# First layer of a four-layer kernel: softmax weights turned by VectorE in 32x32 blocks, values as 32x64 tiles, four engines in a written order

## The chip, the cores and the metric

The kernel runs on one core of one Trainium2 chip. Its engines work side by side and meet through semaphores: TensorE (PE in the profile, with its weight loads shown apart as PEld), VectorE (DVE), ScalarE (ACT), GpSimd (POOL), and the queues that start transfers, of which SyncE (SP) does nothing else. The metric is the time of one execution on the device in microseconds. Three runs of the kernel before gave 3634.38, 3636.60 and 3638.72 us, so the median is 3636.6 us.

## The reference, cut to what matters

Four layers are computed one after the other for a batch of eight sequences. The change touches the first layer only. For each batch b it has two inputs x[b] and ctx[b], read as 256 channels by 512 positions. Queries, keys and values of 16 heads with 64 channels each are linear maps of x and ctx, by matrices of which each is made of blocks that act on the two halves of the positions. Then, per head:

```
scores = (q + r_w_bias)^T k          # 512 x 512, per head
probs  = softmax(scores / 8, over keys)
av     = v probs^T                   # 64 x 512, per head
z      = Wo [av of 16 heads] + bo + x    # 256 x 512
out    = (z - mean) * rsqrt(var + eps)   # over the 256 channels
```

The result of each batch is stored in DRAM and read by the second layer. All arithmetic is fp32.

## The kernel before, in words

`stage_l0` (from line 117) does the first layer. The unit of work is a **pair**: two heads (128 rows of channels) of one batch. There are 8 batches x 8 pairs = 64 pairs. A pair has 512 queries, cut into four quarters of 128; two quarters are a slot, so the layer has 128 slots.

**Groups.** The linear maps are computed by a Strassen-like scheme: a group makes q and k of one pair (kind "qk", 8 per batch) or a quarter of v of one batch (kind "v", 4 per batch). A group has four parts. `load_w` (line 146) issues two transfers of 512 KB. `weight_sums` (line 220) makes four sums of weight blocks, s1 and s3 on POOL (lines 233, 234), s2 and s4 on DVE (235, 236). `group` (257) and `group2` (268) run seven products on TensorE into PSUM banks, four in `group` and three in `group2`, and combine them by additions on DVE and POOL (lines 261 to 298). Each fp32 matmul stands in the trace as two matmul instructions with a weight load each.

**Softmax.** `scores` (300) makes, for each quarter, two matmuls (line 308), the negated row maximum (DVE, 312), its scaling by 1/8 (DVE, 313), two exponentials with row sums (ACT, 317), the reciprocal (DVE, 322) and the scaling of both heads (POOL, 324).

**Turning.** The values need the weights with keys on the partitions. `transposes` (330) turns 128x128 blocks on TensorE against an identity (338) into PSUM, and `evac` copies them to SBUF, alternately on DVE (174) and ACT (172).

**Values.** `values` (343) runs, per slot, eight fp32 matmuls with 128 keys as contraction, two heads side by side in the columns of the array (352); DVE copies the result to SBUF (356). `out_proj` (358) follows once per batch, then the norm (`norm_sum`, `norm_mean`, `norm_var`) and `store`.

**Order.** Only TensorE's order is written by hand: the loop at line 452 runs the scores of the next slot, the values of the last one, pieces of other groups taken from a list with due positions (`Filler`, `put_group`), and the transposes of this slot. The other engines' order is chosen by the framework. The transfers of weights go through SP's queue. In the last slots of the layer, the first steps of the second layer (`g.middle.fill`) are mixed in.

PSUM has eight banks: two score tiles of two banks each (tag "s"), and four banks with the tag "mm" that products, transposes, values and projections share in turn.

Of the kernel before, what the change touches and what calls it, by code (L numbers as in the profile page):

```python
# [116 lines left out]
def stage_l0(g, pools):  # L117
# [11 lines left out]

    nc, tc, I = g.nc, g.tc, g.I  # L130
# [15 lines left out]
    def load_w(kind, b, i, ts=(0, 1), eng=nc.sync):  # L146

        for t in ts:
            shape = [P, 4, ST, P] if kind == "qk" else [P, 2, ST, 256]
            w = g.wpool.tile(shape, F32, tag="w", name="w" + kind)  # L150
            raw.setdefault((kind, b, i), []).append(w)
            eng.dma_start(out=w, in_=I["wqk"][i, t] if kind == "qk" else I["wv"][i // 2, i % 2, t])
# [9 lines left out]
    nc.scalar.dma_start(out=WoT, in_=I["WoT"].rearrange("(k p) o -> p k o", p=P))  # L162
# [3 lines left out]
    qs, ks, vs, avs, sms, pts = {}, {}, {}, {}, {}, {}  # L166
# [10 lines left out]
    def qk_first(b, pr, t):  # L177
# [10 lines left out]
        if t == 0:  # L188
            q = qs[b, pr] = wk.tile([P, L], F32, tag="q", name="q", bufs=2)
            nc.vector.tensor_scalar(q, pp, g.pv("rwb", pr), None, ALU.add)  # L190
        else:
            k_ = ks[b, pr] = wk.tile([P, L], F32, tag="k", name="k", bufs=2)
            nc.scalar.copy(k_, pp)

    def act_sums(b):

        z, u = (x.rearrange("p k (h i l) -> p i k h l", h=2, i=2) for x in (X[b], us[b]))
        t = {n: wk.tile([P, ST, 2, P], F32, tag="ts", name=f"t{n}", bufs=8) for n in (1, 2, 3, 4)}
        sub = lambda e, *a: tc.keep_in_program_order(e.tensor_tensor(*a, ALU.subtract))
        for e, n, x, y in (  # L200
            (nc.gpsimd, 1, z[:, 1], z[:, 0]), (nc.gpsimd, 3, u[:, 1], z[:, 1]),
            (nc.vector, 2, u[:, 1], t[1]), (nc.vector, 4, u[:, 0], t[2]),
        ):
            for k in range(ST):
                sub(e, t[n][:, k], x[:, k], y[:, k])
                yield
# [13 lines left out]
    def weight_sums(kind, b, i):  # L220
# [11 lines left out]
        s1, s2, s3, s4 = (wk.tile(shape, F32, tag="ws", name=f"s{n}", bufs=7) for n in (1, 2, 3, 4))  # L232
        nc.gpsimd.tensor_tensor(s1, a21, a22, ALU.add)
        nc.gpsimd.tensor_tensor(s3, a11, a21, ALU.subtract)
        nc.vector.tensor_tensor(s2, s1, a11, ALU.subtract)
        nc.vector.tensor_tensor(s4, a12, s2, ALU.subtract)
# [20 lines left out]
    def group(kind, b, i):  # L257
# [7 lines left out]
        nc.vector.tensor_tensor(u2, b2[:, 1], s15[:, 0], ALU.add)  # L265
        groups[kind, b, i] = out, s15, u2

    def group2(kind, b, i):
# [3 lines left out]
        x, y = s15[:, 0], wk.tile([P, 256], F32, tag="u3", name="u3", bufs=1)  # L272
        nc.gpsimd.tensor_tensor(x, u2, s15[:, 1], ALU.add)
        nc.vector.tensor_tensor(y, b3[:, 0], u2, ALU.add)
        add(kind, i, out[1], b3[:, 1], x, True)
        add(kind, i, out[2], b4[:, 0], y, False)
        add(kind, i, out[3], y, s15[:, 1], False, nc.gpsimd)

    def blocks(kind, b, i):

        if kind == "qk":
            q = qs[b, i] = wk.tile([P, L], F32, tag="q", name="q", bufs=2)
            k_ = ks[b, i] = wk.tile([P, L], F32, tag="k", name="k", bufs=2)
            return [
                t.rearrange("p (h i l) -> p i h l", h=2, i=2)[:, j] for t in (q, k_) for j in range(2)
            ]
        if i % 2 == 0:
            vs[b, i // 2] = wk.tile([P, 4, 512], F32, tag="vT", name="vT", bufs=2)
        t = vs[b, i // 2]
        return [t[:, 2 * (i % 2) + j, o * 256 : o * 256 + 256] for o in range(2) for j in range(2)]  # L290

    def add(kind, i, out, x, y, biased, eng=nc.vector):
        if kind == "qk":
            x, y = (t.rearrange("p (h l) -> p h l", h=2) for t in (x, y))
# [5 lines left out]
    def scores(b, pr, hf):  # L300
        out = []
        for j in range(2):
            it = 2 * hf + j
            ic = slice(it * P, (it + 1) * P)
            sp = ps.tile([P, 2, L], F32, tag="s", name="sp", bufs=2)
            for h in range(2):
                r = slice(h * DH, (h + 1) * DH)
                nc.tensor.matmul(  # L308
                    sp[:, h, :], lhsT=qs[b, pr][r, ic], rhs=ks[b, pr][r, :], start=True, stop=True
                )  # L310
            nmax = sm.tile([P, 2], F32, tag="nmax", name="nmax")
            nc.vector.tensor_reduce(nmax, sp, AX.X, ALU.max, negate=True)  # L312
            nc.vector.tensor_scalar(nmax, nmax, 1.0 / DH ** 0.5, None, ALU.mult)  # L313
            pe = wk.tile([P, 2, L], F32, tag="pe", name="pe", bufs=4)
            ssum = sm.tile([P, 2], F32, tag="ssum", name="ssum")
            for h in range(2):
                nc.scalar.activation(  # L317
                    pe[:, h, :], sp[:, h, :], AF.Exp, bias=nmax[:, h : h + 1], scale=1.0 / DH ** 0.5,
                    accum_out=ssum[:, h : h + 1],
                )  # L320
            rinv = sm.tile([P, 2], F32, tag="rinv", name="rinv")
            nc.vector.reciprocal(rinv, ssum)  # L322
            for h in range(2):
                nc.gpsimd.tensor_scalar(  # L324
                    pe[:, h, :], pe[:, h, :], rinv[:, h : h + 1], 1.0, ALU.mult, ALU.mult
                )
            out.append(pe)
        sms[b, pr, hf] = out

    def transposes(b, pr, hf, h):  # L330
        pes = sms[b, pr, hf]
        pt = pts[b, pr, hf, h] = wk.tile([P, 4, 2, P], F32, tag="pt", name="pt", bufs=3)
        for j2 in range(2):
            tp = ps.tile([P, 2, 2, P], F32, tag="mm", name="tp", bufs=4)
            for j in range(2):
                jt = 2 * j2 + j
                for i in range(2):
                    nc.tensor.transpose(  # L338
                        tp[:, j, i, :], pes[i][:, h, jt * P : (jt + 1) * P], g.ident
                    )  # L340
            evac(pt[:, 2 * j2 : 2 * j2 + 2], tp)

    def values(b, pr, hf):
        pt = [pts.pop((b, pr, hf, h)) for h in range(2)]
        if hf == 0:
            avs[b, pr] = wk.tile([P, L], F32, tag="av_sb", name="av_sb", bufs=8)
        av = ps.tile([P, 256], F32, tag="mm", name="av", bufs=4)
        vT = vs[b, pr // 4]
        for jt in range(4):
            for h in range(2):  # L350
                col = (2 * (pr % 4) + h) * DH
                nc.tensor.matmul(  # L352
                    av[h * DH : (h + 1) * DH, :], lhsT=vT[:, jt, col : col + DH],
                    rhs=pt[h][:, jt].rearrange("p i c -> p (i c)"), start=(jt == 0), stop=(jt == 3),
                )
        nc.vector.tensor_copy(avs[b, pr][:, hf * 256 : hf * 256 + 256], av)  # L356

    def out_proj(b, mt):
        zb = X[b]
        op = ps.tile([P, L], F32, tag="mm", name="op", bufs=4)  # L360
        for p in range(NP):
            nc.tensor.matmul(
                op, lhsT=WoT[:, p, mt * P : (mt + 1) * P], rhs=avs[b, p],
# [3 lines left out]
            zb[:, mt, :], op, g.pv("bo", mt), zb[:, mt, :], ALU.add, ALU.add  # L367
# [4 lines left out]
    def norm_sum(b):  # L372
        zb = X[b]
        rows[b] = wk.tile([P, L], F32, tag="rs", name="zs", bufs=1)
        nc.gpsimd.tensor_tensor(rows[b], zb[:, 0, :], zb[:, 1, :], ALU.add)

    def norm_mean(b):
# [4 lines left out]
        sq = wk.tile([P, ST, L], F32, tag="sq", name="sq", bufs=1)  # L382
        for k in range(ST):
            nc.vector.tensor_tensor(zb[:, k, :], zb[:, k, :], mp, ALU.subtract)
            nc.gpsimd.tensor_tensor(sq[:, k, :], zb[:, k, :], zb[:, k, :], ALU.mult)
        nc.gpsimd.tensor_tensor(sq[:, 0, :], sq[:, 0, :], sq[:, 1, :], ALU.add)
        rows[b] = sq[:, 0, :]

    def norm_var(b):
# [3 lines left out]
        rs = wk.tile([P, L], F32, tag="rs", name="rs", bufs=1)  # L393
        nc.scalar.activation(rs, vp, AF.Ln, bias=g.eps)
        nc.scalar.activation(rs, rs, AF.Exp, scale=-0.5)
        for k in range(ST):
            nc.gpsimd.tensor_tensor(zb[:, k, :], zb[:, k, :], rs, ALU.mult)
# [5 lines left out]
    def slot(b, pr, hf):  # L403
        return (b * NP + pr) * 2 + hf
# [4 lines left out]
    def put_group(at, *of):  # L409
        if of not in raw:  # L410
            fill.put(at - 6, lambda: load_w(*of))
        fill.put(at - 1.4, lambda: weight_sums(*of))
        fill.put(at + 0.2, lambda: group(*of))
        fill.put(at + 0.5, lambda: group2(*of))

    for b in range(B):
        s = slot(b, 0, 0)
        if b:
            fill.put(s - 13, lambda b=b: load_u(b))
            steps = act_sums(b)  # L420
            for n in range(9):
                fill.put(s - 8.6 + 0.5 * n, lambda steps=steps: next(steps))
            put_group(s - 3, "qk", b, 0)
        put_group(s - (4 if b else 2.8), "v", b, 0)
        put_group(s - (2 if b else 1.4), "v", b, 1)
        for i, at in ((1, -1), (2, 0), (3, 3), (4, 5), (5, 7), (6, 9), (7, 11)):
            put_group(s + at, "qk", b, i)
        put_group(s + 4, "v", b, 2)
        put_group(s + 6, "v", b, 3)
        for mt in range(ST):  # L430
            fill.put(slot(b + 1, 0, 1) + 0.2 + 0.2 * mt, lambda b=b, mt=mt: out_proj(b, mt))
        fill.put(slot(b + 1, 1, 0) + 0.4, lambda b=b: norm_sum(b))
        fill.put(slot(b + 1, 2, 0) + 0.4, lambda b=b: norm_mean(b))
        fill.put(slot(b + 1, 3, 0) + 0.4, lambda b=b: norm_var(b))
        fill.put(slot(b + 1, 4, 0) + 0.4, lambda b=b: store(b))
# [1173 lines left out]
```

## Time and profile before

| what | before |
|---|---|
| median of three runs | 3636.6 us |
| the profiled execution's own time | 3634.69 us |
| its span | 3632.9 us |
| granted TensorE clock, mean | 0.982 |
| first scores matmul (line 308) / last values matmul (line 352) start | 28.1 / 1480.3 us |
| time of one batch in the steady part | 183.0 us |
| in such a batch: PE, DVE, POOL, ACT busy | 183.0, 117 to 119, 106 to 108, 74 us |
| transferred in that part | 79 to 81 GB/s; in the first 50 us 233 GB/s |

The page of the profile gives busy shares per engine, the span in 40 slices, and groups of instructions by line. In a row of a group stand the line, the engine, the operation, what is written and read, the count, then the busy time and the mean duration of one, and at the end the idle time of the engine before them with what released it. The durations of neighbouring instructions overlap, so the pace of a stretch is read from the starts in the timeline, not from the mean duration.

### The profile page before, as it was taken

What the parts mean: (1) busy time and instruction counts of PE and PEld (TensorE: products, weight loads), DVE (VectorE), ACT (ScalarE), POOL (GpSimd) and SP (SyncE); (2) the same over time, 40 slices, a digit from 0 to 9 for tenths busy, and PEclk for the clock granted to TensorE, in tenths of its full rate; (3) what the DMA queues carried; (4) which work ended last, traced back from release to release, by engine and by line L of the source; (5) the groups of instructions that cost most, each with busy time, mean ns of one, the idle gap of its engine ahead of it and who ended that gap; (6) DMA issues with size and microseconds to landing.
All of it is one profiled execution on the core that took longest, in us unless ns stands there. A gap on an engine that the chain in (4) does not pass through costs nothing. (4 is left out here: it accounts for less than half of the span.)

```text
span 3632.9 us, 58189 instructions
## 1 busy us (share of the span) xinstructions
PE 3488.5 (96%) x22144; PEld 2500.9 (69%) x22144; DVE 2455.5 (68%) x3982; ACT 1495.9 (41%) x3616; POOL 2298.9 (63%) x2236
## 2 busy tenths in 40 slices
PE   8999999999999999889999998799999999899999
PEld 6777777777777777556666665466666666589996
DVE  5766575656565666488888887655676777677771
ACT  3434343434343434323333343355566665433222
POOL 5656565646464645356666566566777877688882
PEclk9999999999999999989999999899999999999999
DMA  4222222222222221212332223121121112300002
GB/s 170 85 86 82 76 82 76 83 71 84 73 82 76 82 65 47 93 58 64 111 99 93 91 95 110 53 80 62 55 70 56 52 48 73 114 1 1 1 7 87
DMA packets 102566, 263.13 MB, mean 72 GB/s; under 512 B 8400, under 2 KB 16464, under 8 KB 102288
## 3 DMA queue, kind: packets, MB, share of 16 engines
q1 hardware_dynamic: 98640, 252.21, 21.5%
q10 hardware_dynamic: 2992, 5.37, 0.4%
q8 instruction: 177, 2.90, 0.3%
q0 software_dynamic: 656, 1.81, 0.2%
q14 instruction: 101, 0.83, 0.1%
HBM read 238.39 MB, written 20.97 MB: 71 GB/s over the span
## 5 line engine op out<-in xcount | busy, mean ns | idle before, releaser
L324 POOL TENSOR_SCALAR pe<-pe,rinv 128x512 f32<-128x512 f32 x512 | 386.2, 766 | 466.7 <-DVE nmax L313 411.5
L317 ACT ACTIVATE pe<-sp,nmax 128x512 f32<-128x512 f32 x512 | 347.1, 683 | 601.7 <-DVE nmax L313 597.3
L793 POOL TENSOR_TENSOR rs<-a,r 128x1024 f32<-128x1024 f32 x128 | 303.2, 2384 | 261.1 <-DVE a L788 228.1
L1006 ACT ACTIVATE pe<-pe,nmax 128x256 f32<-128x256 f32 x512 | 253.7, 497 | 194.7 <-DVE nmax L999 194.0
L312 DVE TENSOR_REDUCE nmax<-sp 128x2 f32<-128x1024 f32 x256 | 310.8, 1214 | 8.9 <-PE sp L308 7.9
L1013 POOL TENSOR_SCALAR pe<-pe,rinv 128x256 f32<-128x256 f32 x512 | 236.9, 484 | 115.3 <-DVE rinv L1011 114.5
L788 DVE TENSOR_TENSOR_SCAN a<-w,vb 128x1024 f32<-128x1024 f32 x128 | 287.4, 2275 | 4.8
L308 PE MATMUL sp<-k,q 64*128 64x512 f32 x1024 | 254.7, 615 | 0.2 <-ACT pe L317 0.2
L338 PE MATMUL tp<-ident,pe 128*128 128x128 f32 x2048 | 249.8, 274 | 3.3 <-DVE av_sb L356 1.8
L352 PE MATMUL av<-pt,vT 128*64 128x256 f32 x2048 | 249.3, 385 | 0.0
L172 ACT COPY pt<-tp 128x512 f32<-128x512 f32 x256 | 147.7, 589 | 246.2 <-PE tp L338 246.2
L338 PEld LDWEIGHTS tp<-ident,pe 128*128 128x128 f32 x2048 | 227.1, 141 | 25.2 <-issue 14.8
L352 PEld LDWEIGHTS av<-pt,vT 128*64 128x64 f32 x2048 | 135.7, 136 | 151.6 <-DVE k L298 42.4
L999 DVE TENSOR_REDUCE nmax<-pe 128x4 f32<-128x1024 f32 x128 | 156.1, 1220 | 101.0 <-POOL pe L997 97.5
L249 PE MATMUL gp<-t,s 128*128 128x128 f32 x1512 | 204.9, 278 | 1.4 <-DVE vT L298 1.4
L249 PEld LDWEIGHTS gp<-t,s 128*128 128x128 f32 x1512 | 183.7, 192 | 5.6 <-DVE vT L298 1.6
L997 POOL TENSOR_TENSOR pe<-pe,lconstb 128x1024 f32<-128x1024 f32 x64 | 149.7, 2357 | 50.7 <-DVE pe L990 50.7
L322 DVE RECIPROCAL rinv<-ssum 128x2 f32<-128x2 f32 x256 | 42.4, 166 | 205.6 <-ACT pe L317 205.4
L174 DVE COPY pt<-tp 128x512 f32<-128x512 f32 x256 | 166.2, 679 | 1.5 <-PE tp L338 1.5
L1024 PE MATMUL tp<-ident,pe 128*128 128x128 f32 x1024 | 143.3, 287 | 23.1 <-POOL pe L1013 19.0
L997 POOL TENSOR_TENSOR pe<-pe,mb 128x1024 f32<-128x1024 f32 x64 | 149.7, 2361 | 18.1 <-DVE pe L990 18.1
L784 DVE TENSOR_TENSOR vb<-vb,k 128x1020 f32<-128x1020 f32 x128 | 157.2, 1228 | 4.4
(314 smaller groups left out, 8229.6 us busy)
## 6 DMA issues: line engine op xcount, KB each, us to landing
wqk<-in_wqk_dram SPq DMA_DIRECT2D x127, 512.0 KB, 3.5
wv<-in_wv_dram SPq DMA_DIRECT2D x62, 512.0 KB, 3.5
Wk<-in_l1WkT_dram SPq DMA_DIRECT2D x16, 512.0 KB, 4.1
Wv<-in_l1WvT_dram SPq DMA_DIRECT2D x16, 512.0 KB, 3.9
Wr<-in_l1WrT_dram SPq DMA_DIRECT2D x16, 512.0 KB, 4.2
Wg<-in_l1WgT_dram SPq DMA_DIRECT2D x16, 512.0 KB, 4.5
Wo<-in_l1WoT_dram SPq DMA_DIRECT2D x16, 512.0 KB, 4.2
fWk<-in_l1fWkT_dram SPq DMA_DIRECT2D x16, 512.0 KB, 4.2
```

Source lines behind the costliest of these rows:

```text
L249: nc.tensor.matmul(out[:, hf * P : (hf + 1) * P], lhsT=w[n](hf, k), rhs=a[n](hf, k), start=k == 0, stop=k == ST - 1,)
L308: nc.tensor.matmul(sp[:, h, :], lhsT=qs[b, pr][r, ic], rhs=ks[b, pr][r, :], start=True, stop=True)
L312: nc.vector.tensor_reduce(nmax, sp, AX.X, ALU.max, negate=True)
L317: nc.scalar.activation(pe[:, h, :], sp[:, h, :], AF.Exp, bias=nmax[:, h : h + 1], scale=1.0 / DH ** 0.5, accum_out=ssum[:, h : h + 1],)
L324: nc.gpsimd.tensor_scalar(pe[:, h, :], pe[:, h, :], rinv[:, h : h + 1], 1.0, ALU.mult, ALU.mult)
L338: nc.tensor.transpose(tp[:, j, i, :], pes[i][:, h, jt * P : (jt + 1) * P], g.ident)
L352: nc.tensor.matmul(av[h * DH : (h + 1) * DH, :], lhsT=vT[:, jt, col : col + DH], rhs=pt[h][:, jt].rearrange("p i c -> p (i c)"), start=(jt ...
L788: nc.vector.tensor_tensor_scan(a.rearrange("p n l -> p (n l)"), w4.rearrange("p n l -> p (n l)"), vb[:, 4 * n2 : 4 * n2 + 4, :].rearrange( ...
L793: nc.gpsimd.tensor_tensor(rs, a, rb, ALU.mult)
L997: nc.gpsimd.tensor_tensor(pe4, pe4, b4, ALU.add)
L1006: nc.scalar.activation(pe[:, r, :], pe[:, r, :], AF.Exp, bias=nmax[:, r : r + 1], accum_out=ssum[:, r : r + 1],)
L1013: nc.gpsimd.tensor_scalar(pe[:, r, :], pe[:, r, :], rinv[:, r : r + 1], 1.0, ALU.mult, ALU.mult)
```

## The change

It rewrites what lies between scores and output projection, and the order of the layer.

- `transposes` is gone. `turn` runs one VectorE instruction per quarter: it turns each 32x32 block of the [128, 1024] tile in place of blocks, into SBUF. Row block r of 32 partitions then holds, for its own 32 queries of each quarter, the keys of one block of 32 on the partitions.
- k is written with its positions permuted (`blocks`, `add`, `qk_first`), so that a block of 32 keys is every sixteenth key.
- `values` works on a whole pair: for 16 key blocks, 4 row groups and 2 heads one fp32 matmul with 32 keys, 64 channels and 4 x 32 queries. The four row groups write four PSUM banks, all that the tag "mm" has, and four copies (two on DVE, two on ACT) bring them to SBUF.
- Each row group needs all keys on its own 32 partitions. So v goes to DRAM (`store_v`) and `load_v` reads 256 KB four times per pair.
- Softmax is cut into `scores`, `exp`, `norm`, `norm2`. The scaling of the maximum moves to ACT. Head 0 is scaled by POOL, head 1 by ACT.
- The weight sums s2 and s4 move from DVE to POOL, in two steps. The output projection runs in halves of 256 columns. One small tile (u3) is gone; s15 still has one buffer.
- TensorE, VectorE, ScalarE and GpSimd all run in the order in which the program issues. Positions in the list are thirds of a pair (24 to a batch). The load of WoT moves from ACT's queue at the start to SP's queue at position 9.9.

```diff
+        nc.gpsimd.tensor_tensor(s2, s1, a11, ALU.subtract)
...
+        nc.gpsimd.tensor_tensor(s4, a12, s2, ALU.subtract)
...
+    def norm():
+        pe, ssum, of = exps.pop(0)
+        rinv = sm.tile([P, 2], F32, tag="rinv", name="rinv")
+        nc.vector.reciprocal(rinv, ssum)
+        nc.gpsimd.tensor_scalar(pe[:, 0, :], pe[:, 0, :], rinv[:, 0:1], 1.0, ALU.mult, ALU.mult)
+        halves.append((pe, rinv, of))
+
+    def norm2():
+        pe, rinv, of = halves.pop(0)
+        nc.scalar.mul(pe[:, 1, :], pe[:, 1, :], rinv[:, 1:2])
+        probs.append((pe, of))
+
+    def turn():
+        pe, (b, pr, it) = probs.pop(0)
+        if it == 0:
+            pts[b, pr] = wk.tile([P, 4, 2, L], F32, tag="pt", name="pt", bufs=1)
+        nc.vector.transpose(pts[b, pr][:, it], pe)
...
+    def load_v(b, pr):
+        vr = vrs[b, pr] = wk.tile([P, 16, P], F32, tag="vr", name="vr", bufs=2)
+        for r in range(4):
+            tc.keep_in_program_order(nc.sync.dma_start(
+                out=vr[32 * r : 32 * r + 32],
+                in_=vd[b, pr // 4][pr % 4].rearrange("(k n) c -> k n c", n=16),
+            ))
+
+    def values(b, pr):
+        pt, vr = pts.pop((b, pr)), vrs.pop((b, pr))
+        av = [ps.tile([P, 4, 32], F32, tag="mm", name="av", bufs=4) for _ in range(4)]
+        for kb in range(16):
+            for r in range(4):
+                rows_ = slice(32 * r, 32 * r + 32)
+                for h in range(2):
+                    nc.tensor.matmul(
+                        av[r][h * DH : (h + 1) * DH], lhsT=vr[rows_, kb, h * DH : (h + 1) * DH],
+                        rhs=pt[rows_, :, h, 32 * kb : 32 * kb + 32], start=(kb == 0), stop=(kb == 15),
                     )
...
+        for r in range(4):
+            evac(t.rearrange("p (i r q) -> p r i q", i=4, r=4)[:, r], av[r])
...
     for n, at in enumerate(every):
...
+        nxt, t = every[n + 1] if n + 1 < len(every) else None, 3 * n
+        exp()
+        norm()
+        norm2()
+        turn()
+        fill.until(t + 1.5)
+        if nxt:
+            for it in range(2):
+                scores(*nxt, it)
+                exp()
+            norm()
+        values(*at)
+        if nxt:
+            norm2()
+            norm()
+            norm2()
+            scores(*nxt, 2)
+            exp()
+            turn()
+            turn()
+            fill.until(t + 2.2)
+            norm()
+        fill.until(t + 2.5)
+        if nxt:
+            norm2()
+            scores(*nxt, 3)
+            turn()
+        fill.until(t + 2.95)
...
-    with stack, tc.manual_schedule(engines={mybir.EngineType.PE}):
+    every = {getattr(mybir.EngineType, n) for n in ("PE", "DVE", "Activation", "Pool")}
+    with stack, tc.manual_schedule(engines=every):
         stage_l0(g, pools)
```

## The prediction

> **What bounds the kernel now.** I read the page first, then the busy time of three successive batches, then the groups by line, then the timeline of one slot, and last one short stretch of the second layer.
>
> ```profile
> PE 3488.5 (96%) x22144; PEld 2500.9 (69%) x22144; DVE 2455.5 (68%) x3982; ACT 1495.9 (41%) x3616; POOL 2298.9 (63%) x2236
> PE   8999999999999999889999998799999999899999
> ...
> 213.00:396.00 183.00, 182.90 (x1240) 134.28 (x1238) 119.35 (x239) 74.09 (x176) 107.61 (x126) 1.00 0.26 81
> 396.00:579.00 183.00, 183.00 (x1242) 134.45 (x1240) 117.18 (x238) 74.12 (x176) 105.64 (x122) 1.00 0.25 79
> ```
>
> The columns of the last two lines are stretch, length, then PE, PEld, DVE, ACT and POOL busy, granted clock, transfer share and GB/s. A batch of the first layer takes 183.0 us, and TensorE is busy for all of it at full clock. The others have 64 us or more to spare, so a microsecond off TensorE's work is a microsecond off the batch, until something else is late.
>
> ```profile
> L324 POOL TENSOR_SCALAR pe<-pe,rinv 128x512 f32<-128x512 f32 x512 | 386.2, 766 | 466.7 <-DVE nmax L313 411.5
> L312 DVE TENSOR_REDUCE nmax<-sp 128x2 f32<-128x1024 f32 x256 | 310.8, 1214 | 8.9 <-PE sp L308 7.9
> L338 PE MATMUL tp<-ident,pe 128*128 128x128 f32 x2048 | 249.8, 274 | 3.3 <-DVE av_sb L356 1.8
> L172 ACT COPY pt<-tp 128x512 f32<-128x512 f32 x256 | 147.7, 589 | 246.2 <-PE tp L338 246.2
> L174 DVE COPY pt<-tp 128x512 f32<-128x512 f32 x256 | 166.2, 679 | 1.5 <-PE tp L338 1.5
> ```
>
> These rows price what goes and what is near to what comes. TensorE's pace is read from starts, in the timeline of one stretch:
>
> ```profile
> 401.19 1.91 PE L338 MATMUL tp<-ident,pe 128*128 128x128 f32 x16
> 402.94 1.13 PE L249 MATMUL gp<-t,s 128*128 128x128 f32 x8
> 403.90 1.06 PE L249 MATMUL gp<-u,s 128*128 128x128 f32 x8
> 404.80 1.06 PE L249 MATMUL gp<-t,wqk 128*128 128x128 f32 x8
> 405.79 1.99 PE L308 MATMUL sp<-k,q 64*128 64x512 f32 x8
> 407.70 1.95 PE L352 MATMUL av<-pt,vT 128*64 128x256 f32 x16
> 409.58 0.70 PE L362 MATMUL op<-av_sb,WoT 128*128 128x512 f32 x1
> ```
>
> A slot's transposes take 402.94 - 401.19 = 1.75 us, its scores 1.91, its values 1.88. Eight instructions of 128 columns take 0.90 us, so 0.112 each.
>
> **TensorE.** Sixteen slots of a batch: scores 30.6, transposes 28.0, values 30.1. The other 183.0 - 88.7 = 94.3 us (groups, projection, norm) stay; halving the projection doubles its 16 matmuls over the same columns, under 0.2 us. The new batch is 124.9 + 8V, V being one pair's values. In V, every tile of 32 rows by 64 columns gets 16 blocks x 2 passes = 32 instructions of 128 columns. If the eight tiles run together, V is 32 x 0.112 = 3.6 us and 0.2 to fill and drain: **3.8**, as much as the two slots' values cost now. The batch is 155.3, and the gain the transposes' 28.
>
> What could feed it too slowly is the supply: 512 instructions, half of them weight loads, in 3.6 us, or 7 ns each. No stretch before asks for that for so long. The nearest is the second layer's line 762, four row tiles after a blocked wait:
>
> ```profile
> 1921.31:1921.40 0.09, 0.03 (x4) 0.06 (x4) 1.00 0.00 0
> 1921.40:1921.64 0.24, 0.24 (x4) 0.24 (x8) 1.00 0.00 0
> ```
>
> (Stretch, length, PE and PEld busy of that line alone.) Four matmuls and four weight loads start within the 0.09 us after the wait ends, at most 11 ns each; afterwards the array sets the pace. [...] I take 3.8 by the row, with up to 5.6 (512 x 11 ns) in the range; V = 7.3 is where TensorE's gain is gone ((183.0 - 124.9) / 8).
>
> **VectorE.** Removed per batch: 32 copies of line 174 (20.8 us busy), 32 scalings of line 313 (5.9), the sums of lines 235 and 236 (21.6: 8 x (1.04 + 0.71) + 4 x (1.15 + 0.74)), 16 copies of line 356 (6.7). Added: 32 transposes and 16 evacuations of 128x128, some 0.29 each from line 356's 0.417 for 256. The transpose is in no row. One pass over 1024 elements costs 1.21 us in line 312. [...] Low end 0.6 (half of line 312). I take **1.21**, the nearest row. [...]
>
> **ScalarE and GpSimd.** ACT loses line 172 (18.5) and gets 32 scalings of the maximum at 0.20 (line 61), 32 of head 1 at 0.63 (line 395) and 16 evacuations at 0.28: 74 - 18.5 + 31 = 86. POOL loses 32 of 64 scalings (24.1) and gets 24 sums at 1.28 (lines 233, 234): 106 - 24 + 31 = 113. None reaches 155, so busy time alone leaves TensorE the bound.
>
> **Transfers.** Per batch 32 loads of 256 KB and eight stores come to SP's queue: 8.4 + 2.1 MB on 14.5. 25 MB in 160 us is 156 GB/s; the first 50 us moved 233. A store waits on SP for POOL's last addition of a v group, and behind it wait the next weight and v loads. Weights are issued 7 thirds of a pair ahead (4.3 for two groups), v loads 3.9, over 20 us, and a 512 KB load lands in 3.5. Cost nothing; without that cover each late load would stall a pair by about 4. WoT's 1 MB leaves the start, where POOL waits 9.1 us for wv: up to 4 us gained there, offset by v's trip through DRAM before the first values.
>
> **The written order.** This is what I expect to bind. The values of a pair need all four quarters turned and all four "mm" banks empty, and each of four engines stops at its first unready instruction. I followed one pair along VectorE. Work: four maxima and four turns 9.7, reciprocals 0.7, one and a half groups 3.3, evacuations 0.6, less overlap: 13.8. Waits: (1) from quarter 3's maximum to its turn lie scaling 0.2, exponentials 1.45 (408.60 to 410.05 in the timeline), reciprocal 0.17, POOL 0.77 and hand-overs 0.3, covered only by one turn: 1.5. Behind that turn stand the additions that empty the banks, for which the values wait. (2) Quarter 0's exponentials, 1.65 behind a maximum of 1.21: 0.6. (3) Quarter 1's, which start after those, with two evacuations as cover: 1.0. (4) ACT's scalings of head 1 before the turns: 0.5. (5) s15 has one buffer, so in every second pair ACT's copy waits for POOL's last addition of the group before: 1.3, on average 0.65. Together **18.1 us** a pair, 145 a batch, above TensorE's 17.7 in the pairs without projection ((155.3 - 13.8) / 8). The first two pairs of a batch carry 6.9 us of projection each on TensorE: 24.5 against 18.1, so 12.8 more. The norm's table loads (2 x 1.28 on ACT) and its POOL work: 4. Batch: **162**. I put the unknown of these waits at -7 (all covered) to +25 a batch.
>
> **Sum.** Eight batches: 8 x (162 - 183) = -168. The second layer's first steps, near the layer's end, put some 17 us on VectorE (20 at 0.47, 4 at 0.86, a subtraction, statistics), no longer free: +12. Start and tail: +8. Total -148 on the profiled execution's 3634.7, which lies 1.9 below the median: 3486.7 there, **3489 us** for the runs. A run can tell about 0.2%, 7 us.
>
> **Rivals.**
> 1. *The order hides everything; TensorE stays the bound.* For it: 40 us of slack per engine. Against: the five waits, most with only one instruction as cover. 8 x (155.3 - 183) = -222, +8: 3423.
> [...]
> [...]
> 4. *No change*: V and waits eat just 28 a batch.
>
> **How the numbers follow.** Forecast 0.47, its own range 3445 to 3570; rival 1 0.22; rival 2 0.15; rival 3 0.13; rival 4 0.03. Faster 0.69, same 0.03, slower 0.28. The range 3405 to 3690 holds forecast, rivals 1 and 4 and the near part of 2 and 3; some 0.17 lies above it.
>
> **What would show it.** Right: no matmuls of line 338; the values of a pair start to end in 3.7 to 4.2 us; VectorE's transpose near 1.2 us; TensorE busy 90 to 97% of a batch of 155 to 170, its idle time before the values, released by VectorE, and before banks freed by ACT. Wrong: values of 7 us or more; transposes of 2 us and more; TensorE idle behind v loads; waits of 5 us and more a pair.

## The result, and the profile after

The changed kernel takes 3667.1 us (median of four runs, 3660.7 to 3674.6) against 3637.2 for the kernel before in the same comparison. The ratio is 1.0084, with a 95% interval of 1.0064 to 1.0104: **slower by 0.84%**. The forecast was 3489 us and faster. The profiled execution took 3667.9 us, its span is 3666.2.

The page of the kernel after: the sum of each engine, TensorE in 40 slices, its granted clock, and one row of the transfer queues that I had not read before the prediction (packets, MB, share).

```profile
PE 3362.2 (92%) x34688; PEld 2467.1 (67%) x34688; DVE 2403.6 (66%) x3552; ACT 1600.7 (44%) x4000; POOL 2328.4 (64%) x2170
...
PE   8998898888889898788999998799999999899999
...
PEclk9999999999999999898999999899999999999999
...
q8 instruction: 275, 4.51, 0.5%
```

TensorE lost 126 us of busy time and gained idle time: the nines of the first layer have turned into eights and nines. Before, the row of q8 was:

```profile
q8 instruction: 177, 2.90, 0.3%
```

The 98 packets that came match the matmuls and weight loads that TensorE gained: 2 x (34688 - 22144) = 25088 = 98 x 256. A packet carries 256 instructions.

Two successive batches (columns as in the prediction):

```profile
235.00:418.80 183.80, 165.71 (x2807) 128.46 (x2806) 112.96 (x187) 87.06 (x224) 111.35 (x117) 0.97 0.49 139
418.80:604.30 185.50, 166.46 (x2811) 129.41 (x2810) 111.03 (x183) 87.17 (x224) 109.59 (x115) 0.96 0.47 135
```

TensorE is busy for 166 of 185 us, and its clock is no longer 1.00. The other engines are near what was forecast (VectorE 111 to 113 against the 106 of the prediction's terms, 118 - 55 + 32 x 1.21 + 16 x 0.29; ScalarE 87 against 86, GpSimd 110 to 111 against 113).

The value matmuls before, and then the groups after of the parts that the prediction priced:

```profile
L352 PE MATMUL av<-pt,vT 128*64 128x256 f32 x2048 | 249.3, 385 | 0.0
```

```profile
L392 PE MATMUL av<-pt,vr 32*64 32x128 f32 x16384 | 304.5, 284 | 135.8 <-issue 109.4
...
L363 DVE STREAM_TRANSPOSE pt<-pe 128x1024 f32<-128x1024 f32 x256 | 309.9, 1229 | 75.8 <-POOL pe L351 75.8
...
L181 DVE COPY av_sb<-av 128x128 f32<-128x128 f32 x128 | 31.9, 287 | 198.0 <-PE av L392 197.8
```

VectorE's turn costs 1.229 us, the evacuation 0.287. What the forecast had put at nothing is in the first row: 135.8 us of idle time before the value matmuls (0.0 before the change), 109.4 of it released by "issue". On this page that is time in which the engine waited for nothing that the profile shows: no semaphore, no other engine.

One pair's values in the timeline of TensorE (start, length, then what ran, and the idle time before it in brackets):

```profile
551.70 1.02 PE L324 MATMUL sp<-k,q 64*128 64x512 f32 x4
552.65 2.88 PE L392 MATMUL av<-pt,vr 32*64 32x128 f32 x183
558.83 2.41 PE L392 MATMUL av<-pt,vr 32*64 32x128 f32 x73 [3.30 <-issue]
561.16 1.23 PE L324 MATMUL sp<-k,q 64*128 64x512 f32 x2
```

and the same pair as busy time by stretch:

```profile
552.65:555.20 2.55, 2.55 (x182) 2.55 (x184) 2.36 (x3) 1.25 (x4) 2.47 (x4) 1.00 0.97 336
555.20:558.80 3.60, 0.33 (x21) 0.11 (x7) 0.17 (x1) 1.94 (x7) 3.14 (x4) 0.88 0.97 299
558.80:561.00 2.20, 2.17 (x73) 2.01 (x72) 0.09 (x1) 0.03 (x1) 0.00 (x0) 0.50 0.82 300
```

The first 182 matmuls run in 2.55 us, 14 ns each with their weight load. One after another, at the 0.112 us of an instruction of 128 columns, they would take 20.4 us, eight times as long: the eight tiles do work side by side. Then TensorE stands for more than 3 us, and the last 73 matmuls run at a clock of 0.50 and need 2.2 us. Around the stop the transfer engines are 97% busy with the loads of v and weights, at 300 GB/s.

I numbered TensorE's instructions (matmuls, weight loads and semaphore waits) in the order of the trace. A stop is a distance of over 0.7 us from one start to the next. Up to the last values 64 stops stand at places that are exactly a multiple of 256 apart, 128.5 us together (mean 2.0, 17 of them over 2.5). In the kernel before only ten such distances occur up to the last values, no two of them in step with 256. In the pair above the packet with the next 256 instructions starts at 556.52 and TensorE resumes 2.3 us later. It is so everywhere: at each of the 64 stops TensorE resumes 2.2 to 2.9 us after a packet of q8 has started. Packets never follow each other within less than 3.4 us, which makes 3.4 / 256 = 13 ns an instruction at best. The values ask for one every 7 ns. (Before, no two packets were closer than 12.6 us.)

So **theory A**: TensorE stops at the ends of its 256-instruction blocks because the next block has not come, and the stops cost what was hoped for. **Theory B**, the forecast's own: the written chain of maximum, exponentials, scaling and turn sets the batch, and the stops only fill its slack.

Where a batch's time went, as the mean of six middle batches, in us. I gave the time from one TensorE start to the next to the first of the two, up to its own duration, and the rest to "idle"; the last two columns are experiments that follow.

| | before | after | half the instructions | values cut in two |
|---|---|---|---|---|
| groups | 77.3 | 78.9 | 77.4 | 77.7 |
| scores | 30.7 | 34.2 | 32.3 | 32.7 |
| values | 30.1 | 36.5 | 32.2 | 37.5 |
| transposes | 28.9 | none | none | none |
| projection, norm | 15.8 | 16.0 | 16.0 | 16.0 |
| idle | 0.0 | 19.5 | 4.6 | 14.1 |
| batch | 182.8 | 185.1 | 162.7 | 177.9 |

The transposes' 28.9 us are gone. In their place came 19.5 of idle time, 16.1 of it within the values, and 11.5 more for values, scores and groups.

### The profile page after: what moved, and what is told of

It reads as the page before. It is cut to its first block, busy times and chain, and to the rows that moved or that the text cites. A ratio compares the mean times of both kernels' runs of the same rounds, so it can differ in the third digit from the quotient of the medians.

```text
span 3666.2 us, 83914 instructions
## 1 busy us (share of the span) xinstructions
PE 3362.2 (92%) x34688; PEld 2467.1 (67%) x34688; DVE 2403.6 (66%) x3552; ACT 1600.7 (44%) x4000; POOL 2328.4 (64%) x2170
## 5 line engine op out<-in xcount | busy, mean ns | idle before, releaser
L392 PE MATMUL av<-pt,vr 32*64 32x128 f32 x16384 | 304.5, 284 | 135.8 <-issue 109.4
L392 PEld LDWEIGHTS av<-pt,vr 32*64 32x64 f32 x16384 | 261.5, 136 | 209.3 <-issue 141.8
L351 POOL TENSOR_SCALAR pe<-pe,rinv 128x512 f32<-128x512 f32 x256 | 177.7, 695 | 316.1 <-DVE rinv L350 315.7
L363 DVE STREAM_TRANSPOSE pt<-pe 128x1024 f32<-128x1024 f32 x256 | 309.9, 1229 | 75.8 <-POOL pe L351 75.8
L324 PE MATMUL sp<-k,q 64*128 64x512 f32 x1024 | 286.2, 655 | 24.3 <-POOL k L317 19.1
L333 ACT ACTIVATE nmax<-nmax 128x2 f32<-128x2 f32 x256 | 51.7, 202 | 435.5 <-DVE nmax L328 435.5
L265 PEld LDWEIGHTS gp<-t,s 128*128 128x128 f32 x1512 | 189.3, 197 | 40.0 <-issue 20.4
L356 ACT ACTIVATE pe<-pe,rinv 128x512 f32<-128x512 f32 x256 | 178.3, 723 | 43.0 <-DVE rinv L350 43.0
L282 POOL TENSOR_TENSOR s<-u,s 128x256 f32<-128x256 f32 x95 | 69.3, 729 | 157.6 <-DVE u L281 157.6
L1106 PE MATMUL tp<-ident,pe 128*128 128x128 f32 x1024 | 143.6, 287 | 20.8 <-POOL pe L1095 16.9
L181 DVE COPY av_sb<-av 128x128 f32<-128x128 f32 x128 | 31.9, 287 | 198.0 <-PE av L392 197.8
```

Source lines behind the costliest of these rows:

```text
L265: nc.tensor.matmul(out[:, hf * P : (hf + 1) * P], lhsT=w[n](hf, k), rhs=a[n](hf, k), start=k == 0, stop=k == ST - 1,)
L324: nc.tensor.matmul(sp[:, h, :], lhsT=qs[b, pr][r, ic], rhs=ks[b, pr][r, :], start=True, stop=True)
L356: nc.scalar.mul(pe[:, 1, :], pe[:, 1, :], rinv[:, 1:2])
L363: nc.vector.transpose(pts[b, pr][:, it], pe)
L392: nc.tensor.matmul(av[r][h * DH : (h + 1) * DH], lhsT=vr[rows_, kb, h * DH : (h + 1) * DH], rhs=pt[rows_, :, h, 32 * kb : 32 * kb + 32], s ...
```

## The experiments

The first three have one run each, the others four to twelve, beside runs of the kernel before.

**Half the instructions, the same array work.** Each value matmul takes 256 columns and only 8 of the 16 key blocks are computed.

```diff
-        av = [ps.tile([P, 4, 32], F32, tag="mm", name="av", bufs=4) for _ in range(4)]
-        for kb in range(16):
+        av = [ps.tile([P, 4, 64], F32, tag="mm", name="av", bufs=4) for _ in range(4)]
+        for kb in range(8):
...
-                        rhs=pt[rows_, :, h, 32 * kb : 32 * kb + 32], start=(kb == 0), stop=(kb == 15),
+                        rhs=pt[rows_, :, h, 64 * kb : 64 * kb + 64], start=(kb == 0), stop=(kb == 7),
```

> The values of a pair run with half the instructions and the same columns: 8 key blocks instead of 16, each with 256 query columns instead of 128. The other 8 key blocks are left out, so the sums are not those of the reference. Theory A (TensorE's instructions arrive in blocks of 256, and a pair's 512 outrun their fetch): few stops inside the values, a pair's values 3.6 to 4.3 us instead of 6.4 in the median, in all about 3667 - 122 (the stops) - 25 (the clock that falls after them) = 3520, between 3480 and 3560. Theory B (the written order and its waits set the pair, the values' length does not matter): 3630 or more. Theory C (eight tiles do not run together): the values keep 6 us and more, total as after.

Measured: 3500.0 us. The page and the stretch from 235 to 1400 us:

```profile
q8 instruction: 211, 3.46, 0.4%
...
L392 PE MATMUL av<-pt,vr 32*64 32x256 f32 x8192 | 275.1, 389 | 27.9 <-DVE pt L363 8.6
```

```profile
235.00:1400.00 1165.00, 1109.96 (x12218) 831.88 (x12215) 766.70 (x1261) 606.23 (x1553) 732.54 (x758) 0.98 0.51 144
```

There are 64 packets fewer, 16384 / 256. Of the stops at block ends two are left (4.6 us), the values last 3.45 us in the median from first to last start instead of 6.44, and a batch takes 162.7. All the rest of the change, written order, turns, v through DRAM, is still in it. The loss is thus the value instructions' number, not their arithmetic. (Half of the weight loads went too. That the stream counts, and not the weight loads, follows from the places of the stops, and from the cut further down, which leaves every instruction in.)

**Half the array work, the same instructions.** Only two of the four query quarters are computed, with 64 columns a matmul.

```diff
-        av = [ps.tile([P, 4, 32], F32, tag="mm", name="av", bufs=4) for _ in range(4)]
+        av = [ps.tile([P, 2, 32], F32, tag="mm", name="av", bufs=4) for _ in range(4)]
...
-                        rhs=pt[rows_, :, h, 32 * kb : 32 * kb + 32], start=(kb == 0), stop=(kb == 15),
+                        rhs=pt[rows_, 0:2, h, 32 * kb : 32 * kb + 32], start=(kb == 0), stop=(kb == 15),
```

> The same 512 instructions per pair, each with 64 query columns instead of 128: quarters 2 and 3 of the queries are left out and get copies of quarters 0 and 1. The array's work in the values is halved, 1.8 us less a pair. Theory A: the fetch sets the length, a pair's values stay at 5 us or more and the total between 3600 and 3670. Theory C (the array sets it): values near half, 3.2 us, total 3550 or less.

Measured: 3703.7 us, above the range and slower than with all the work. TensorE's waits from 60 to 1480 us (sum, times, longest), then the stretch from 235 to 1400:

```profile
PE av L392 <- issue: 146.9, 65, 6.1
```

```profile
235.00:1400.00 1165.00, 1011.13 (x17184) 783.96 (x17183) 681.82 (x1118) 532.06 (x1371) 669.12 (x700) 0.91 0.47 133
```

With half the work TensorE stands longer at the ends of its blocks (71 stops, 174.7 us, against 64 and 128.5), and the granted clock over this stretch is 0.91 instead of 0.97. The size of the array work doesn't set the values' time. A lower clock was in neither of the two theories of this run.

**The values twice.** The 16 key blocks are gone through two times, 1024 instructions a pair; the sums are double.

```diff
-        for kb in range(16):
+        for k2 in range(32):
+            kb = k2 % 16
...
-                        rhs=pt[rows_, :, h, 32 * kb : 32 * kb + 32], start=(kb == 0), stop=(kb == 15),
+                        rhs=pt[rows_, :, h, 32 * kb : 32 * kb + 32], start=(k2 == 0), stop=(k2 == 31),
```

> The values' stream twice in a row per pair, 1024 instructions, so the result is twice the reference's values. Theory A: a stream that long runs at the fetch's pace. The shortest spacing of two fetches after the change is 3.4 to 3.5 us, so 512 more instructions cost 6.9 us a pair and the total is about 3667 + 64 x 6.9 = 4110, between 4050 and 4170. If only the array counted, it would be 64 x 3.6 more: 3900.

Measured: 4156.9 us.

```profile
q8 instruction: 403, 6.60, 0.7%
```

128 packets more for 32768 instructions, again 256 each. A pair's values take 14.45 us or 14.1 ns an instruction, with 169 stops of 344 us in all. The added 512 instructions cost (4156.9 - 3667.1) / 64 = 7.7 us a pair. This is the pace of the supply in a long stream.

**No loads of v.** After the first two pairs, v isn't loaded again; each pair uses one of the first two tiles instead of its own, and 62 x 1 MB of transfers are gone. Nothing else changes.

```diff
+        if (b, pr) > (0, 1):
+            vrs[b, pr] = kept[pr % 2]
+            return
         vr = vrs[b, pr] = wk.tile([P, 16, P], F32, tag="vr", name="vr", bufs=2)
+        kept.append(vr)
```

> v is loaded for the first two pairs only and these two tiles serve all pairs: 62 MB of loads are left out, and the values are wrong for all other pairs. Theory A1 (part of the stops is the fetch queueing behind v and weight data; after the change a block came back in 3.1 to 3.5 us with no data moving and in 5 to 6 us with 1.3 to 1.6 MB moving): the stops over 2.5 us go, 30 to 50 us off, 3615 to 3640. Theory A2 (the traffic costs nothing, the fetch's latency is the same): 3655 to 3675.

Measured: 3637.5 us, ratio to the kernel before 1.0002 (0.9993 to 1.0010).

```profile
PE av L398 <- issue: 87.6, 53, 3.7
```

(TensorE's waits, 60 to 1480 us; after had 109.4.) The loads cost 30 us, and not by coming late: in the trace of after no value matmul waits for one. Without them the stops at the ends of blocks shrink: there are 55 of 105 us instead of 64 of 128.5, and 10 instead of 17 of them are over 2.5 us. (The trace is of the slowest of the twelve runs, 3650.3 us; the stops are 23 us of the gain, the rest is not accounted for.) In the trace of after it can be followed packet by packet. In the 47 stops of up to 2.5 us the packet that was missing had started 0.9 us (median) after TensorE entered the block before; in the 17 longer ones it started 2.3 to 4.0 us after. Over all blocks of the layer, the next packet starts 2.6 us (median of 66) after TensorE enters a block where the transfer engines were over 80% busy with data in the first microsecond, and 1.0 us (median of 96) where they were under 20% busy. Without the loads the change would still bring nothing.

**Work put between the two halves of the values.** If theory A holds, it should help to cut the stream into two pieces of 256 instructions with longer matmuls between. First I put one, then both of the leading score quarters of the next pair there, with nothing left out (the diff is of the second; in the first, the scores of quarter 0 stay ahead of the values):

```diff
-    def values(b, pr):
+    def values(b, pr, mid=None):
...
+            if kb == 8 and mid:
+                mid()
...
-        if nxt:
+        def mid():
             for it in range(2):
                 scores(*nxt, it)
                 exp()
             norm()
-        values(*at)
+        values(*at, mid if nxt else None)
```

> Same work as after the change; the scores of the next pair's quarter 1 are issued between key blocks 8 and 9 of the values instead of before them. Theory A (the values wait for the fetch of a block of 256 instructions, once in most pairs): 0.95 us of other work with few instructions lies inside the block that is being waited for, so up to 0.95 us of each stop is covered: 60 us off, 3590 to 3625. If the stops were of another kind, moving the scores gains nothing: 3655 to 3690, as quarter 1's maximum comes later.

Measured: 3661.8 us (ratio 1.0070, 1.0052 to 1.0088), 5 us below after, which the two intervals do not tell apart.

> Same work; the scores of the next pair's quarters 0 and 1 are both issued between key blocks 8 and 9 of the values. Theory A: 1.9 us of work with few instructions covers most of a stop (2.0 us in the mean): 64 x 1.65 = 105 off, some 20 more by the clock, up to 20 lost because the maxima come 1.8 us later: 3560, between 3530 and 3610, faster than the kernel before. Theory B (the order of VectorE's work sets the pair): later maxima make it slower, 3680 or more.

Measured: 3708.6 us (1.0197, 1.0180 to 1.0214), slower than after. Theory A's times failed in both runs, and the times of its rivals came (3655 to 3690, and 3680 or more), though the stops went as theory A says: 28 of 58 us in the first, 9 of 18 in the second. In the first, the six middle batches idle 6 us less each, but the values take 40.6 instead of 36.5 and the scores 36.0 instead of 34.2, and TensorE's waits for the sums of a group (lines 277, 281, 317) in the values rise from 14.4 to 23.7 us over the layer. The second shows plainly what happens. One pair of the second in the timeline:

```profile
532.21 0.43 PE L394 MATMUL av<-pt,vr 32*64 32x128 f32 x4 [0.21 <-issue]
532.91 0.43 PE L394 MATMUL av<-pt,vr 32*64 32x128 f32 x4 [0.26 <-issue]
534.30 2.44 PE L394 MATMUL av<-pt,vr 32*64 32x128 f32 x120 [0.96 <-issue]
536.67 1.99 PE L324 MATMUL sp<-k,q 64*128 64x512 f32 x8
538.59 2.10 PE L394 MATMUL av<-pt,vr 32*64 32x128 f32 x128
```

The brackets name no releaser, but the starts at 532.88 (weight loads) and 534.27 follow within 0.1 us the ends of VectorE's additions of the group (line 281 at 532.80, line 315 at 534.20). Another pair as stretches:

```profile
763.90:766.20 2.30, 1.20 (x12) 0.61 (x12) 1.77 (x5) 0.00 (x0) 1.56 (x2) 0.97 0.98 212
766.20:769.50 3.30, 3.30 (x119) 3.28 (x116) 0.00 (x0) 0.00 (x0) 3.22 (x4) 0.51 1.00 345
```

and TensorE's waits for the group's sums in the values (sum, times, longest), from 60 to 1480 us:

```profile
PE av L394 <- ACT s L277: 26.1, 23, 1.1
PE av L394 <- DVE vT L317: 14.2, 15, 1.7
PE av L394 <- DVE u L281: 13.6, 21, 1.5
```

They are 53.9 us together, against 14.4 in after. The second half of the values now runs in its 2.1 us without a stop. The first half doesn't: its first four matmuls, one bank, run, and the next banks come one by one. The scores that stood ahead of the values had been the time in which the group's "mm" banks were emptied, and I had moved that cover away. Then 119 matmuls run at a clock of 0.51. The first half lasts 4.8 us instead of 1.8 (medians). The maxima of the next pair start later as well (theory B); what of the loss is theirs I did not separate. This cut is no clean test of theory A.

**The same with later loads.** The second of these, with `load_v` due 1.3 positions before its pair instead of 2.4.

```diff
-            fill.put(s + 3 * pr - (2.4 if b or pr else 4), lambda b=b, pr=pr: load_v(b, pr))
+            fill.put(s + 3 * pr - (1.3 if b or pr else 4), lambda b=b, pr=pr: load_v(b, pr))
```

> As with two quarters inside, and v's loads are issued after a pair's values (position 1.7 of the pair instead of 0.6), so that fewer of them move while the values run. Theory A1 (data ahead of the fetch makes the long stops): 10 to 25 us below the run with two quarters inside, about 3545. If the place of the loads does not matter: the same within 7 us.

Measured: 3697.4 us (1.0164, 1.0149 to 1.0180), 11 us below the version with the earlier loads. The size is what A1 said, the way is not: there are 12 stops of 19.3 us instead of 9 of 18.1, though none over 2.5 us, and what became shorter is the first half of the values (4.4 us instead of 4.8, medians). Why is not shown.

**Only TensorE's order by hand.** The changed kernel, with the order of the other three engines left to the framework as before.

```diff
-    every = {getattr(mybir.EngineType, n) for n in ("PE", "DVE", "Activation", "Pool")}
+    every = {getattr(mybir.EngineType, n) for n in ("PE",)}
```

> The change with only TensorE in written order; the framework orders VectorE, ScalarE and GpSimd as it did before the change. Theory A (the fetch is what the change lost, the written order costs or gains little): 3640 to 3700. Theory B (the written order is itself a cost): below 3630. Theory D (the written order is what carries the change): 3720 or more.

Measured: 3658.8 us (1.0060, 1.0045 to 1.0075), 8 us below after, which the two intervals hardly tell apart, with as many stops (65, 127.8 us). The hand-written order of VectorE, ScalarE and GpSimd is not what costs, nor does it gain here.

**A cut that keeps the cover.** Now quarters 0 and 1 stay ahead of the values, and quarter 2, which had followed them, goes between the halves.

```diff
+            if kb == 8 and mid:
+                mid()
...
-        values(*at)
+        values(*at, (lambda: scores(*nxt, 2)) if nxt else None)
         if nxt:
             norm2()
             norm()
             norm2()
-            scores(*nxt, 2)
             exp()
```

> As after, but the two score matmul pairs of the next pair's third query block stand in the middle of the values (after key block 8) instead of behind them; the two pairs ahead of the values stay, so the PSUM banks of the group sums have the same time to come free as before. Theory A (instruction supply: a stream of 512 instructions in one piece stops at a 256-instruction boundary, two streams of 256 with 1.5 us of longer matmuls between stop less): the stops fall from 128 us to some 40 to 70 us in all, and the time to 3585 to 3630 us. Theory B (the chain scores, maxima, exponentials, normalisation sets the batch, and the stops only fill its slack): the stops turn into waits elsewhere and the time stays at 3645 to 3680 us. If the third block's scores wait for a score buffer (0.5 us a pair), 30 us of A's gain is lost.

Measured: **3619.6 us**, ratio to the kernel before 0.9954 (0.9940 to 0.9968): 47.5 us below after, and below the kernel before. TensorE's waits from 60 to 1480 us, then one pair in its timeline:

```profile
PE av L394 <- issue: 32.4, 26, 3.4
PE sp L324 <- ACT pe L337: 25.5, 52, 3.4
...
PE gp L265 <- DVE av_sb L181: 13.9, 48, 0.4
```

```profile
943.76 1.02 PE L324 MATMUL sp<-k,q 64*128 64x512 f32 x4
944.71 2.09 PE L394 MATMUL av<-pt,vr 32*64 32x128 f32 x128
946.97 1.13 PE L324 MATMUL sp<-k,q 64*128 64x512 f32 x4 [0.16 <-ACT pe L337]
948.03 2.44 PE L394 MATMUL av<-pt,vr 32*64 32x128 f32 x128
```

The wait for "issue" falls from 109.4 to 32.4 us, the stops from 64 to 23 (40.6 us). Both halves take 1.83 us (medians). Some of the gain is given back as expected: quarter 2's scores wait 25.5 us for a score buffer.

Was it the cut, or that quarter 2 starts earlier? **The same scores after key block 12** still start earlier than in after, but leave streams of 384 and 128 instructions.

```diff
-            if kb == 8 and mid:
+            if kb == 12 and mid:
```

> As the kernel with the third block's scores after key block 8 of the values, but they stand after key block 12: streams of 384 and 128 instructions instead of two of 256. The maxima of the third block begin 0.9 us later than there and still some 1.5 us earlier than in after. Theory A (what gained was that the stream is cut in two halves): 384 instructions cross two boundaries of 256 in one of two pairs, so the stops come back to 70 to 110 us in all, and the time is 3635 to 3655 us. Theory B (what gained was that the third maximum starts earlier): the gain shrinks only by the later start, at most 0.9 us in the pair, a third of what separates the two kernels: 3620 to 3637 us, whatever the stops do.

Measured: 3658.9 us (1.0057, 1.0040 to 1.0074), four us above theory A's range and far from theory B's.

```profile
PE av L394 <- issue: 72.6, 51, 5.2
```

There are 43 stops of 82.8 us. Moving the cut by four key blocks takes back 39 of the 47.5 us, and the stops grow by 42. It is the length of the unbroken stream that counts.

**Later loads, and the framework's order, on top of the cut after key block 8.** First the later loads alone:

> As the kernel with the third block's scores in the middle of the values, and the four loads of the values' operand are issued later (due time 1.3 instead of 2.4 before the pair), behind the values of the pair before. Theory A: 8 to 15 us below that kernel, since less data moves while the instruction blocks are fetched. Theory B: within 5 us of it.

Measured: 3624.8 us (0.9971, 0.9961 to 0.9982), 5 us above the cut alone, with 24 stops of 47.4 us instead of 23 of 40.6. Theory A's gain did not come. The 5 us are what theory B allowed, and the two intervals overlap: with the stream cut, the place of the loads no longer matters much. Then the framework's order as well:

> As the kernel with the scores in the middle and the later loads, but only TensorE keeps the written order; VectorE, ScalarE and GpSimd are ordered by the framework. From the run of that edit on its own (8 us below after): 5 to 10 us below the kernel without it; Theory B, with the chain as the bound, would make this the edit that matters: 15 us and more either way.

Measured: 3759.3 us (1.0343, 1.0327 to 1.0358), 135 us above the kernel with the later loads. Theory B named the size, but most of the loss is another wait than its chain of maxima. Of TensorE's waits from 60 to 1480 us:

```profile
PE gp L265 <- DVE av_sb L181: 107.5, 47, 2.6
```

With quarter 2 no longer between values and groups, the group's products follow the values at once and need their banks. The framework's order has VectorE copy these out late: its first copy starts 2.1 us (median) after the end of the values, by hand at once. By hand TensorE waits 13.6 us for it, so this wait makes 94 of the 135 us, and here the written order is worth having. What makes the rest was not separated.

## Why the prediction was wrong

- **The failed step is the supply, and with it V = 3.8.** V was 6.44 us, in the median and in the mean, which is 21 of the 30 us by which TensorE's batch was too short (155.3 against 185.1). I read the pace of 512 instructions from a burst of eight (at most 11 ns each). The burst was right for what it showed: half a pair runs at 7 ns an instruction, 1.82 us for 256. What I left out is the step from one block to the next: the instructions come 256 to a packet (25088 more of them in 98 more packets), 64 stops stand at the ends of blocks, and a long stream gets 14.1 ns an instruction (the values twice). Of V, 2.1 us are idle time (135.8 / 64: 1.7 released by "issue", 0.4 by others); two halves at full pace need 3.6, and the other 0.7 are slower matmuls. The packets of row q8 were the view to read: a pair's values need two in 3.8 us, and before the change no two were closer than 12.6.
- **Transfers "cost nothing" was wrong by 30 us** (no loads of v: 3637.5). I asked only whether a load comes late, and none did. It is the instruction blocks, which come through a queue too, that came later: the next packet starts 2.6 us after TensorE enters a block where the transfer engines are busy with data, and 1.0 where they are not. Where the two meet no run isolates.
- **The batch of 162 was right in size.** With the instructions halved it is 162.7, so the sum without the failed term stood. But the reason was partly another, so the agreement is partly luck: TensorE's own work there is 158 us, not 155.3 (values 4.0 a pair instead of 3.8, scores 1.6 a batch more), and it idles 4.6, not 6.7. I expected VectorE's chain with its five waits, 18.1 us a pair, to bind; TensorE waited for a turn only three times in that run (8.6 us). The order hides nearly all of it, as rival 1 had it. Two of the waits do not follow from their own terms either: the first adds up to 2.9 less 1.2, which is 1.7 and not 1.5, and the second is 1.65 - 1.21 = 0.44 and not 0.6; the two slips cancel.
- **From 155 to 185:** TensorE's batch was put at 124.9 + 8V, which is 176.4 at V = 6.44. Measured 185.1. Of the other 8.7 us, 4.2 are scores, groups and projection that run slower (129.1 instead of 124.9), 3.4 are idle time outside the values, and 1.1 is the last value matmul of each pair: V ends at its start, and the values with their idle time take 52.6 a batch, not 51.5.
- **The sum of the rest held.** Start, tail and the second layer's first steps were put at +20. The span grew by 33.3 us, and eight batches at 2.4 more (185.1 - 182.75) make 19 of it, so 14 are left. With the instructions halved the span is 134.7 below before, eight batches make -160, and 26 are left. After the change they lie in the first and the last batch: from the first scores of the first batch to those of the second pass 182.2 us instead of 170.6, and from the first scores of the last batch to the last values 194.8 instead of 185.3. Against that the first scores start 3.6 us earlier (24.5 instead of 28.1; up to 4 was forecast).
- **The turn** took 1.229 us (forecast 1.21). Evacuations 0.287 (0.29) held, and the busy times 111 to 113, 87, 110 to 111 (106, 86, 113) came near.
- **Rivals 2 and 3** (chances 0.15 and 0.13, and the upper end of the range) rest on prices, of an instruction in the values and of a turn, that no run shows. What the runs showed in their place: 7 ns an instruction within half a pair, 14.1 ns in a long stream, with V = 6.44 and the loss in stops at the ends of blocks (64 of them, 128.5 us) and not at every instruction; and 1.229 us a turn. The kernel did get slower, and the values were the place.
- **V = 7.3**, where TensorE's gain was to be gone, was too high: at 6.44 it was gone already, because the rest of TensorE's work took 129.1 us a batch instead of 124.9, the values 52.6 instead of 8 x 6.44 = 51.5, and 3.4 of idle time outside the values came on top.

## What to carry to other kernels

Before splitting matmuls into small tiles, count instructions per microsecond: a stream that asked for one every 7 ns outran the fetch, which here sustained 256 in 3.4 to 3.6 us, while pieces of 256 with longer matmuls between them largely ran through (23 stops instead of 64). Idle time released by "issue" (109.4 us), at places 256 instructions apart, was the sign, and interleaving work with few instructions was the cure here (3667.1 to 3619.6 us), as long as the work that is moved was not the cover for something else. Heavy data transfers in the same microseconds went with longer stops (the next packet came 2.6 instead of 1.0 us after a block began).

## What the runs showed of the hardware that was not expected

- Long stops were followed by a lower clock. In after, 14 of the 17 stops over 2.5 us were followed by a mean granted clock under 0.9 in the next 2.2 us, and none of the 41 up to 2.0 us; in before the clock was never lowered between 60 and 1480 us. The length of the stop is not all: with half the array work, 15 of 22 stops of up to 2.0 us were followed so too, and the stretch from 235 to 1400 us had 0.91 on average, but 0.95 with the values twice, which has more stops. What the clock goes by stays open. Halving the array's work made the kernel slower (3703.7 against 3667.1, one run).
- Eight tiles of 32 rows by 64 columns ran together: 182 matmuls of 128 columns in 2.55 us, 14 ns each; in before an instruction of 128 columns took 112 where they run one after another.
- The shortest distance between two instruction packets was 3.2 to 3.4 us in all twelve runs with at least 512 value instructions a pair, with and without the loads of v. A packet of 16 KB takes 1.0 us itself (median, after), so its own time does not fill the distance. In the trace of after the distance has two parts: TensorE resumes at the earliest 2.2 us after the start of the packet that it lacked, and the next packet starts at the earliest 1.0 us after TensorE has resumed. So at none of the 64 stops did the packet after the missing one start while TensorE stood. What fills the 2.2 us beside the packet stays open.
